# Sparse graph attention: shorter upper slot layers for eleven node tiles

## Chip, cores and metric

The kernel runs on one core of one Trainium2 chip. The metric is the device time of one execution in microseconds (us). The engines are PE (matrix multiply), DVE (vector), ACT (scalar, activation), POOL (GpSimd) and SP (sync, which only issues transfers here).

## What is computed

The input is `x` (4096 nodes, 128 features, float32) and an adjacency matrix `adj` (4096 x 4096, int32) with about 32 neighbours in a row. Two layers follow one another:

```
# layer 0: graph attention, 8 heads
Wh  = einsum('nd,hde->hne', x, W);  f1, f2 = Wh.a1, Wh.a2
e   = leaky_relu(f1[:, :, None] + f2[:, None, :], 0.2)
att = softmax(where(adj > 0, e, -9e15))
h   = elu(einsum('hnm,hmd->hnd', att, Wh))
x1  = layernorm(x + elu(concat_heads(h) @ W1 + b1))
# layer 1: per node and feature, quantiles (0.25, 0.5, 0.75) of x1
# over the kept neighbours, mean of the three, half mixed with x1, a linear layer, residual
```

Only the pairs where `adj` is set matter, so the kernel turns each row of `adj` into a list of neighbour numbers and fetches the rows that it needs.

## The kernel before

**Search.** `neighbours` (L550 and after) reads `adj` in tiles of 128 nodes, two loads of 1 MB each, makes keys from it on ACT and PE (L568, L607, L610), and takes the largest keys with DVE's MAX8 (L574, L579, L581). What comes out for a node is a record: 64 neighbour numbers, their count, the node's own number, `f1`, and the features. The work of one search is cut into pieces that are run between the parts of other work.

**Blocks.** The 32 tiles of nodes go through search and attention in three blocks of 4, 9 and 19 tiles (`BLOCKS`). Within a block the nodes are ranked by their neighbour count (`rank_by_count`, last instruction L750), and their records are scattered by rank into a DRAM array `recs_d` with one indirect transfer for each tile (L187, `rec_d<-rec,ranks`). A tile that is read back from there holds 128 nodes of nearly the same count, in rising order. While block b is in attention, the search of block b+1 runs between; its ranks are needed by the scatters that are placed among the last fetches of block b (`among` in `fetch_rows`).

**Slots and layers.** `CAPS` gives the largest count that each tile is laid out for. `layers(cap)` rounds it up to a multiple of 4 and splits it into layers of width 32, 16, 8 or 4. A layer of width w holds w slots of each of the 128 nodes; the 128 partitions of one gather then stand for 128/w nodes with w slots each, and w gathers cover the tile. A tile thus takes as many gathers as it has slots, each an indirect transfer of 128 rows of 136 floats (L178, `G<-xt_d,idx`) that POOL starts.

**Preparing a tile.** `read_lists` loads the tile's records `R` with four transfers by SP (L786), compares the count with the cap (L787; any node over it sets `bad`, and a general path then runs after all), and makes for each layer the index tile `idx` and the spread `f1x` on DVE. A layer of width 32 is transposed straight from `R` (L798). A narrower layer first gets four more transfers by SP into a buffer `narrow` (L806), one buffer for each width, then a copy `ids` (L808), a transpose (L811), a copy `f1b` (L815, the last reader of `narrow`) and a transpose `f1x` (L820).

**A step.** `step` handles one tile position i: it issues the fetch of tile i to POOL, runs `attend` for tile i-1 and the tail of `attend` for tile i-2, prepares tile i+2 after the first part of `attend`, and runs search pieces between the parts. The engines run in the order of the program text, so an instruction that waits holds all that follow it on its engine. `attend` adds `f1x` to the fetched scores (L869), exponentiates (L876), sums by node on PE (L883, `small`), takes the reciprocal (L894), spreads it back on PE (L898, `rz`), and for each layer builds the weights `wide` (L914) and multiplies the fetched rows by them, one matmul for each gather (L926, `y`). L883 and L898 take 32/w matmuls for a layer of width w. The fetched rows stand in a ring of six buffers `G` of 16 gathers; a buffer is free again when the `y` matmuls have read it.

**Layer 1.** After the last tile of attention, all `x1` rows are in DRAM, and POOL gathers neighbour rows again (L178, `vals`), while DVE runs a selection network on them (L1117).

The functions that the change touches:

Of the kernel before, what the change touches and what calls it, by code (L numbers as in the profile page):

```python
# [9 lines left out]
F32 = mybir.dt.float32  # L10
# [3 lines left out]
ALU = mybir.AluOpType  # L14
# [5 lines left out]
P = 128  # L20
N = 4096
D = 128
H = 8
# [20 lines left out]
CAPS = {  # L44
    4: [29, 33, 37, 60],
    9: [26, 28, 30, 32, 33, 35, 37, 40, 61],
    19: [24, 26, 27, 28, 29, 30, 30, 31, 32, 33, 33, 34, 35, 36, 37, 38, 40, 42, 62],
    32: [
        23, 24, 25, 26, 27, 27, 28, 29, 29, 30, 30, 30, 31, 31, 32, 32,
        33, 33, 34, 34, 35, 35, 36, 36, 37, 37, 38, 39, 40, 41, 44, 63,  # L50
    ],
}
BLOCKS = [4, 9, 19]


TURNS = {4: range(4), 9: range(9), 19: [0, 1, 2, 3, 18, 4, 5, 6, 7, *range(9, 18), 8]}

CAP = CAPS[NT]
# [15 lines left out]
R_NUM, R_OWN, R_F1 = L, L + 1, L + 2  # L74
# [10 lines left out]
def layers(c):  # L85


    out = []
    s = 0
    for w in (32, 32, 16, 8, 4):  # L90
        if (c + 3) // 4 * 4 - s >= w:
            out.append((s, w))
            s += w
    return out


def selection_network(n, targets):
# [104 lines left out]
def kernel(  # L202
# [15 lines left out]
    nc = tc.nc  # L218
# [3 lines left out]
    recs_d = [dram.tile([n * P, REC], F32, name=f"rec{n}_d") for n in BLOCKS]  # L222
# [5 lines left out]
    const = ctx.enter_context(tc.tile_pool(name="const", bufs=1))  # L228
# [6 lines left out]
    pidx = const.tile([P, 1], F32, name="pidx")  # L235
# [5 lines left out]
    for w in (32, 16, 8, 4):  # L241
        k = P // w
# [8 lines left out]
    for w in (32, 16, 8, 4):  # L251
        k = P // w // 4
# [13 lines left out]
    bad = const.tile([P, 5, NT], F32, name="bad")  # L266
# [17 lines left out]
    parts = adjp.tile([64, N], BF16, name="parts", bufs=1)  # L284
# [18 lines left out]
    with tc.tile_pool(name="setup", bufs=1) as sp, tc.tile_pool(  # L303
        name="setup_ps", bufs=2, space=PSUM
# [9 lines left out]
    attp = tc.alloc_tile_pool(name="att", bufs=2, reuse_waits="tile")  # L314
# [8 lines left out]
    narrow = {  # L323
        w: attp.tile([P, 32 // w, NARROW[w]], F32, name=f"narrow{w}", bufs=1) for w in NARROW
    }
    for v in narrow.values():
        nc.gpsimd.memset(v, 0.0)

    def prepare(b, i, t0):
        n = BLOCKS[b]  # L330
        i = TURNS[n][i]
        return read_lists(tc, attp, recs_d[b], i, CAPS[n][i], t0 + i, bad, narrow)

    ready = []

# [45 lines left out]
    t0 = 0  # L381
    with tc.manual_schedule(engines=ORDERED):
# [3 lines left out]
        for b, n in enumerate(BLOCKS):  # L386
            last = b == len(BLOCKS) - 1
            if last:
# [4 lines left out]
                idx = keep.tile([P, NT, L], I32, name="idx")  # L393
                cp = tc.alloc_tile_pool(name="cnt_all", bufs=2, side="right", reuse_waits="tile")
                pieces, left = None, 0
            else:
                pieces, left = search(t0 + n, BLOCKS[b + 1]), pieces_of(BLOCKS[b + 1])
            ready.append(prepare(b, 0, t0))
            for i in range(n):
# [6 lines left out]
                if not last and i == n - 1:  # L406
# [3 lines left out]
                    left = 0  # L410
# [12 lines left out]
                if last and i == n - 5:  # L423
                    R = cp.tile([P, NT, REC1], F32, name="R", bufs=1)
# [4 lines left out]
                    left = -(-LIST_PIECES // 4)  # L429
# [14 lines left out]
    with tc.tile_pool(name="sort", bufs=2) as sp, tc.tile_pool(name="fin", bufs=3) as fp, tc.tile_pool(  # L444
        name="fin_ps", bufs=2, space=PSUM
# [329 lines left out]
    return k  # L775


def read_lists(tc, ap, rec_d, i, cap, t, bad, narrow):


    nc = tc.nc

    R = ap.tile([P, REC], F32, name="R", bufs=5)
    rows = rec_d[ts(i, P), :]
    for u in range(4):
        nc.sync.dma_start(R[ts(u, 32), :], rows.rearrange("(g u) w -> u g w", u=4)[u])  # L786
    nc.vector.tensor_scalar(  # L787
        bad[:, 4, t : t + 1], R[:, R_NUM : R_NUM + 1], float(cap), None, ALU.is_gt
    )
    mine = ap.tile([P, 1], I32, name="mine", bufs=9)  # L790
    nc.vector.tensor_copy(mine, R.bitcast(I32)[:, R_OWN : R_OWN + 1])
    f1x32 = None
    parts = []
    for s0, w in layers(cap):
        k, e = P // w, 32 // w
        idx = ap.tile([P, 32], I32, name="idx", bufs=8)
        if w == 32:
            nc.vector.transpose(idx, R.bitcast(I32)[:, s0 : s0 + w])  # L798
            f1s = R[:, R_F1 : R_F1 + H].unsqueeze(1)
        else:  # L800

            v = narrow[w]
            words = R_X - s0
            src = rows.rearrange("(g i e) w -> i g e w", i=4, e=e)
            for j in range(4):
                nc.sync.dma_start(v[32 * j : 32 * j + w, :, 0:words], src[j, :, :, s0:R_X])  # L806
            ids = ap.tile([P, 32], I32, name="ids")
            nc.vector.tensor_copy(  # L808
                ids.rearrange("p (e s) -> p e s", e=e), v.bitcast(I32)[:, :, 0:w]
            )  # L810
            nc.vector.transpose(idx, ids)  # L811
            f1s = v[:, :, words - H : words]
        if w < 32 or f1x32 is None:
            f1b = ap.tile([P, H, 32], F32, name="f1b", bufs=1)
            nc.vector.tensor_copy(  # L815
                f1b.rearrange("p h (e s) -> p h e s", e=e),
                f1s.rearrange("p e h -> p h e").unsqueeze(3).to_broadcast([P, H, e, w]),
            )
            f1x = ap.tile([P, H * 32], F32, name="f1x", bufs=9)
            nc.vector.transpose(f1x, f1b.rearrange("p h g -> p (h g)"))  # L820
            if w == 32:
                f1x32 = f1x
        else:
            f1x = f1x32
        parts.append((s0, w, idx, f1x.rearrange("p (h g) -> p g h", h=H)[:, 0:w, :]))
    return R, mine, parts


def fetch_rows(tc, ap, lists, xt_d, among):

    nc = tc.nc
    R, mine, parts = lists
    out = []
    left = sum(w for _, w, _, _ in parts)
    G, col = None, 16
    for s0, w, idx, f1v in parts:
        runs = []
        for g in range(w):
            if col == 16:
                G, col = ap.tile([P, 16, XW], F32, name="G", bufs=6), 0  # L840
            if not runs or col == 0:
                runs.append([G, col, g, 0])
            runs[-1][3] += 1
            gather(nc, G[:, col, :], xt_d, idx[:, g : g + 1])
            col += 1
            left -= 1
            if among and left % 2 == 0 and left <= 2 * len(among) + 4:
                scatter(nc, *among.pop(0))
        out.append((w, P // w, runs, f1v))
    for v in among:  # L850
        scatter(nc, *v)
    return R, mine, out


def attend(tc, ap, pp, fetched, consts):


    nc = tc.nc
    R, mine, parts = fetched
    own, ownT = consts["own"], consts["ownT"]  # L860
    slots = sum(w for w, _, _, _ in parts)


    z = ap.tile([P, L, H], F32, name="z", bufs=2)
    layer = []
    a = 0
    for w, k, runs, f1v in parts:
        for G, col, g, m in runs:
            nc.vector.tensor_tensor(  # L869
                z[:, a + g : a + g + m, :], G[:, col : col + m, D:], f1v[:, g : g + m, :], ALU.add  # L870
            )
        layer.append(a)
        a += w
    zs = z[:, 0:slots, :].rearrange("p s h -> p (s h)")
    nc.vector.scalar_tensor_tensor(zs, zs, ALPHA, zs, ALU.mult, ALU.max)
    nc.scalar.activation(zs, zs, AF.Exp)  # L876
# [1 line left out]

    small = consts["small"]
    den = small[:, 0 : 32 * H]  # L880
    for i, (w, k, runs, f1v) in enumerate(parts):
        for r in range(k // 4):
            nc.tensor.matmul(  # L883
                den[0:4, :].rearrange("p (g r h) -> p r g h", r=k // 4, h=H)[:, r],
                lhsT=own[w][:, ts(r, 4)],
                rhs=z[:, layer[i] : layer[i] + w, :],
                start=(i == 0 and r == 0),
                stop=(i == len(parts) - 1),
                skip_group_check=True,
            )  # L890
# [2 lines left out]
    nc.vector.tensor_scalar(rden, den[0:4, :], TINY, None, ALU.max)  # L893
    nc.vector.reciprocal(rden, rden)  # L894
    rz = pp.tile([P, L * H], F32, name="rz")
    for i, (w, k, runs, f1v) in enumerate(parts):
        for r in range(k // 4):
            nc.tensor.matmul(  # L898
                rz[:, layer[i] * H : (layer[i] + w) * H],
                lhsT=ownT[w][:, r, :],  # L900
                rhs=rden.rearrange("p (g r h) -> p r g h", r=k // 4, h=H)[:, r],
                start=(i == 0 and r == 0),
                stop=(r == k // 4 - 1),
                skip_group_check=True,
            )
# [2 lines left out]

    y = pp.tile([P, 2, 512], F32, name="y")
    yf = y.rearrange("p a b -> p (a b)")  # L910
    for i, (w, k, runs, f1v) in enumerate(parts):
        pf = ap.tile([P, H * P], F32, name="wide")
        spread = [P, w, k, H]
        nc.vector.tensor_tensor(  # L914
            pf.rearrange("p (g k h) -> p g k h", g=w, k=k),
            z[:, layer[i] : layer[i] + w, :].unsqueeze(2).to_broadcast(spread),
            own[w].unsqueeze(1).unsqueeze(3).to_broadcast(spread),
            ALU.mult,
        )
        yield  # L920
        c = k * H
        for G, col, g0, m in reversed(runs):

            for g in reversed(range(g0, g0 + m)):

                nc.tensor.matmul(  # L926
                    yf[:, ts(g, c)],
                    lhsT=G[:, col + g - g0, 0:D],
                    rhs=pf[:, ts(g, c)],
                    start=(i == 0 and g % (w // 2) == w // 2 - 1),  # L930
                    stop=(i == len(parts) - 1),
                    skip_group_check=True,
                )
                if g % 8 == 0:
                    yield
# [455 lines left out]
```

## Time and profile before

| what | value |
|---|---|
| median of 3 runs | 3857.79 us (3854.88 to 3884.28) |
| profiled execution, own time | 3857.37 us |
| its span, from first to last instruction | 3855.5 us |
| POOL busy | 2807.9 us, 73% |
| DVE busy | 2671.4 us, 69% |
| PE busy | 1253.7 us, 33% |
| gathers `G`, attention | 1180, 947 ns median, 995 ns mean |
| gathers `vals`, layer 1 | 1024, 1382 ns mean |

Times in views of the trace are us from the start of the span. In a list of instructions in time, the columns are start, duration, engine, line, operation, operands, and in brackets how long the engine stood idle before it and what ended that. `issue` as a releaser is time in which the engine waited for nothing that the profile shows. In lists of waits the columns are total us, times and the longest single wait.

### The profile page before, as it was taken

The numbers are of one execution on the slowest core, as the hardware profiler recorded it, in microseconds if no ns is written. First come the engines' busy times: TensorE is split into PE (matmuls) and PEld (weight loads), VectorE is DVE, ScalarE is ACT, GpSimd is POOL, SyncE is SP. The second block draws the span as 40 slices with busy tenths as digits, with TensorE's granted clock in tenths as the row PEclk, the third lists the DMA queues.
The fourth block names the chain that finished last, engine by engine and source line by source line (L and its number), as shares of the span: only waits on it lengthen the run. The fifth ranks groups of instructions, "written<-read, shape, count | busy, mean of one in ns | idle before, by whom it ended". The sixth has DMA issues, their size and how long they took to land. (4 is left out here: it accounts for less than half of the span.)

```text
span 3855.5 us, 21960 instructions
## 1 busy us (share of the span) xinstructions
PE 1253.7 (33%) x5433; PEld 961.2 (25%) x5433; DVE 2671.4 (69%) x6439; ACT 403.4 (10%) x603; POOL 2807.9 (73%) x2388
## 2 busy tenths in 40 slices
PE   6483867863746444455600000000000000000001
PEld 2143534543635444444500000000000000000000
DVE  8774688782522222257436888669999999998788
ACT  3111223210111101111100000000000000000000
POOL 1657674577777777777478888877788887888882
PEclk9975666655665555555555555555555555555555
DMA  6423444322222222222111111111111111111110
GB/s 213 153 88 106 150 139 132 122 54 65 54 55 53 54 53 54 64 58 55 34 47 38 41 39 34 38 42 41 41 38 28 32 35 44 38 35 38 38 40 16
DMA packets 110281, 241.25 MB, mean 63 GB/s; under 512 B 46976, under 2 KB 63360, under 8 KB 101952
## 3 DMA queue, kind: packets, MB, share of 16 engines
q0 software_dynamic: 76160, 160.24, 15.3%
q10 hardware_dynamic: 9360, 67.18, 5.1%
q1 hardware_dynamic: 24624, 12.34, 1.3%
q8 instruction: 45, 0.74, 0.1%
q14 instruction: 92, 0.75, 0.1%
HBM read 228.44 MB, written 11.15 MB: 62 GB/s over the span
## 5 line engine op out<-in xcount | busy, mean ns | idle before, releaser
L178 POOL DMA_INDIRECT vals<-x_d,idx x1024 | 1415.6, 1382 | 314.4 <-issue 303.8
L178 POOL DMA_INDIRECT G<-xt_d,idx x1180 | 1173.6, 995 | 483.4 <-issue 339.9
L1117 DVE TENSOR_TENSOR work<-work 128x256 f32<-128x256 f32 (+7 forms) x1168 | 921.5, 823 | 0.7
L1137 PE MATMUL st_ps<-dg,goal 128*128 128x128 f32 x286 | 71.9, 429 | 1791.9 <-DVE goal L1117 1704.4
L1117 DVE TENSOR_TENSOR work<-work,work 128x512 f32<-128x512 f32 (+4 forms) x820 | 584.3, 738 | 1.3
L1137 PEld LDWEIGHTS st_ps<-dg,goal 128*128 128x128 f32 x286 | 63.7, 324 | 1798.4 <-issue 1797.5
L926 PE MATMUL y<-wide,G 128*128 128x32 f32 (+3 forms) x2360 | 480.1, 382 | 21.9 <-DVE wide L914 21.9
L926 PEld LDWEIGHTS y<-wide,G 128*128 128x128 f32 x2360 | 460.0, 297 | 45.8 <-DVE wide L914 24.2
L869 DVE TENSOR_TENSOR z<-G,f1x 128x128 f32<-128x128 f32 (+2 forms) x92 | 29.9, 335 | 471.6 <-DMA G<-xt_d,idx 468.5
L1117 DVE TENSOR_TENSOR work<-vals 128x768 f32<-128x768 f32 (+11 forms) x64 | 128.8, 2028 | 267.8 <-DMA vals<-x_d,idx 265.7
L574 DVE MAX8 first<-key 128x8 f32<-128x128 f32 x1024 | 227.5, 282 | 112.5 <-PE key L610 112.5
L607 PE MATMUL key<-sgn,markb 128*128 128x512 bf16 x256 | 142.0, 555 | 160.9 <-DVE first L574 107.5
L883 PE MATMUL small<-z,own 128*4 128x32 f32 (+3 forms) x436 | 50.4, 284 | 368.1 <-ACT z L876 368.1
L1136 ACT ACTIVATE dg<-ident,wt 128x128 f32<-128x128 f32 x143 | 47.5, 394 | 1105.0 <-PE st_ps L1137 1104.6
L568 ACT ACTIVATE sgn<-adj_t 128x2048 bf16<-128x2048 int32 x64 | 122.1, 1907 | 343.0 <-PE key L607 328.2
L898 PE MATMUL rz<-rden,ownT 4*128 4x32 f32 (+3 forms) x436 | 107.1, 419 | 117.9 <-DVE rden L894 96.5
L610 PE MATMUL key<-parts,oneb 64*128 64x512 bf16 x256 | 140.6, 550 | 6.3 <-POOL parts L196 6.3
L956 PE MATMUL small<-W_sb,late 128*128 128x128 f32 x512 | 118.9, 426 | 33.6 <-DVE late L953 33.6
L898 PEld LDWEIGHTS rz<-rden,ownT 4*128 4x128 f32 x436 | 94.5, 310 | 134.0 <-DVE rden L894 68.3
L187 POOL DMA_INDIRECT out_dram<-o,own_i x32 | 67.9, 2123 | 79.9 <-ACT o L1163 56.2
L883 PEld LDWEIGHTS small<-z,own 128*4 128x4 f32 x436 | 27.1, 102 | 385.8 <-ACT z L876 373.3
L956 PEld LDWEIGHTS small<-W_sb,late 128*128 128x128 f32 x512 | 110.2, 327 | 44.9 <-DVE late L953 43.9
(179 smaller groups left out, 1879.3 us busy)
## 6 DMA issues: line engine op xcount, KB each, us to landing
adj_t<-in_adj_dram ACTq DMA_DIRECT2D x64, 1024.0 KB
G<-xt_d,idx POOLq DMA_INDIRECT x1180
vals<-x_d,idx POOLq DMA_INDIRECT x1024
R<-rec_d SPq DMA_DIRECT2D x128, 26.2 KB
xt_d<-rec SPq DMA_DIRECT2D x4, 544.0 KB
rec<-in_x_dram SPq DMA_DIRECT2D x4, 512.0 KB
W_sb<-in_L_gnn_W_dram SPq DMA_DIRECT2D x2, 512.0 KB
a_b<-in_L_gnn_a_dram SPq DMA_DIRECT2D x2, 512.0 KB
```

What stands on the lines that cost most here:

```text
L178: nc.gpsimd.indirect_dma_start(out=dst, out_offset=None, in_=rows, in_offset=bass.IndirectOffsetOnAxis(ap=idx, axis=0),)
L187: return nc.gpsimd.indirect_dma_start(out=rows, out_offset=bass.IndirectOffsetOnAxis(ap=idx, axis=0), in_=src, in_offset=None,)
L568: nc.scalar.activation(sgn, adj_t, AF.Sign, accum_out=cnt[:, i : i + 1])
L574: nc.vector.max(first[:, ts(c0 // CW + c, 8)], key[:, ts(c, CW)])
L607: nc.tensor.matmul(key, lhsT=markb, rhs=sgn[:, ts(b, 512)], start=True, stop=False)
L610: nc.tensor.matmul(key, lhsT=oneb[0:64, :], rhs=parts[:, ts(r, 512)], start=False, stop=True)
L883: nc.tensor.matmul(den[0:4, :].rearrange("p (g r h) -> p r g h", r=k // 4, h=H)[:, r], lhsT=own[w][:, ts(r, 4)], rhs=z[:, layer[i] : layer ...
L898: nc.tensor.matmul(rz[:, layer[i] * H : (layer[i] + w) * H], lhsT=ownT[w][:, r, :], rhs=rden.rearrange("p (g r h) -> p r g h", r=k // 4, h ...
L926: nc.tensor.matmul(yf[:, ts(g, c)], lhsT=G[:, col + g - g0, 0:D], rhs=pf[:, ts(g, c)], start=(i == 0 and g % (w // 2) == w // 2 - 1), stop ...
L956: nc.tensor.matmul(o, lhsT=hv[:, h, :], rhs=consts["W1_sb"][:, h, :], start=(h == 0), stop=(h == H - 1))
L1117: nc.vector.tensor_tensor(slots_of(dst, (j, c, s, m), size), slots_of(a, (i, c, s, m), size), slots_of(b, (i + d, c, s, m), size), op,)
L1137: nc.tensor.matmul(st_ps[:, u, :], lhsT=goal[:, (j * k + u) * D : (j * k + u + 1) * D], rhs=dg, start=(j == 0), stop=False,)
```

## The change

A table `LAYERS` gives eleven tiles (block size, tile in the block) a list of layers of their own. Each entry has a third number g0: a layer with g0 > 0 fetches only gathers g0 to w-1, that is, the slots of the tile's last nodes. The other tiles keep `layers(cap)` with g0 = 0. For the adjacency that the reference draws, every node of these tiles has at least as many slots as neighbours.

```diff
+LAYERS = {
+    (4, 1): [(0, 32, 0), (32, 8, 7)],
+    (4, 2): [(0, 32, 0), (32, 4, 0), (36, 8, 7)],
+    (4, 3): [(0, 32, 0), (32, 16, 0), (48, 16, 15)],
+    (9, 0): [(0, 16, 0), (16, 8, 0), (24, 4, 2)],
+    (9, 4): [(0, 32, 0), (32, 4, 1)],
+    (9, 6): [(0, 32, 0), (32, 4, 0), (36, 4, 2)],
+    (9, 8): [(0, 32, 0), (32, 16, 0), (48, 16, 14)],
+    (19, 1): [(0, 16, 0), (16, 8, 0), (24, 4, 1)],
+    (19, 9): [(0, 32, 0), (32, 4, 2)],
+    (19, 17): [(0, 32, 0), (32, 8, 0), (40, 4, 1)],
+    (19, 18): [(0, 32, 0), (32, 16, 0), (48, 16, 13)],
+}
+def steps_of(parts):
+    held = [0] * P
+    for s0, w, g0 in parts:
+        for q in range(g0 * P // w, P):
+            if held[q] == s0:
+                held[q] += w
+    assert held == sorted(held)
+    return held[0], [(q, held[q] - held[q - 1]) for q in range(1, P) if held[q] > held[q - 1]]
...
+    nodeq = const.tile([P, 1], F32, name="nodeq")
+    for u in range(4):
+        nc.gpsimd.memset(nodeq[ts(u, 32), :], -float(P - 1) * u)
+    nc.vector.scalar_tensor_tensor(nodeq, pidx, 4.0, nodeq, ALU.mult, ALU.add)
...
+        parts = LAYERS.get((n, i)) or layers(CAPS[n][i])
...
-    nc.vector.tensor_scalar(
-        bad[:, 4, t : t + 1], R[:, R_NUM : R_NUM + 1], float(cap), None, ALU.is_gt
-    )
+    cap, rises = min(cap, steps_of(layer_list)[0]), steps_of(layer_list)[1]
+    over = R[:, R_NUM : R_NUM + 1]
+    for q, more in rises:
+        up = ap.tile([P, 1], F32, name="up", bufs=3)
+        nc.vector.tensor_scalar(up, nodeq, float(q), -float(more), ALU.is_ge, ALU.mult)
+        nc.vector.tensor_tensor(up, up, over, ALU.add)
+        over = up
+    nc.vector.tensor_scalar(bad[:, 4, t : t + 1], over, float(cap), None, ALU.is_gt)
...
-        for g in range(w):
+        for g in range(g0, w):
...
-        pf = ap.tile([P, H * P], F32, name="wide")
-        spread = [P, w, k, H]
+        k, n = P // w, w - g0
+        pf = ap.tile([P, H * P], F32, name="wide")
+        spread = [P, n, k, H]
```

The sums, the spreading back, the weights and the `y` matmuls of `attend` run over gathers g0 to w-1 in the same way. Each of the eleven tiles has one rise, so its check of the count takes two more small DVE instructions. The slots of these tiles, which are also their gathers, before and after, are:

| tile | widths before | gathers | widths after (gathers kept of the last layer) | gathers |
|---|---|---|---|---|
| (4,1) | 32, 4 | 36 | 32, 8 (1) | 33 |
| (4,2) | 32, 8 | 40 | 32, 4, 8 (1) | 37 |
| (4,3) | 32, 16, 8, 4 | 60 | 32, 16, 16 (1) | 49 |
| (9,0) | 16, 8, 4 | 28 | 16, 8, 4 (2) | 26 |
| (9,4) | 32, 4 | 36 | 32, 4 (3) | 35 |
| (9,6) | 32, 8 | 40 | 32, 4, 4 (2) | 38 |
| (9,8) | 32, 32 | 64 | 32, 16, 16 (2) | 50 |
| (19,1) | 16, 8, 4 | 28 | 16, 8, 4 (3) | 27 |
| (19,9) | 32, 4 | 36 | 32, 4 (2) | 34 |
| (19,17) | 32, 8, 4 | 44 | 32, 8, 4 (3) | 43 |
| (19,18) | 32, 32 | 64 | 32, 16, 16 (3) | 51 |

Tile (19,18) is fetched as the fifth of its block, (19,17) as the last but one.

More of the change, by code (lines that the diff above doesn't have):

```diff
@@ L91, in layers @@
         if (c + 3) // 4 * 4 - s >= w:
-            out.append((s, w))
+            out.append((s, w, 0))
             s += w
     return out
+def steps_of(parts):
[6 more added lines that the diff above has]
+    return held[0], [(q, held[q] - held[q - 1]) for q in range(1, P) if held[q] > held[q - 1]]
 def selection_network(n, targets):
@@ L331, in prepare @@
         i = TURNS[n][i]
-        return read_lists(tc, attp, recs_d[b], i, CAPS[n][i], t0 + i, bad, narrow)
+        parts = LAYERS.get((n, i)) or layers(CAPS[n][i])
+        return read_lists(tc, attp, recs_d[b], i, CAPS[n][i], parts, t0 + i, bad, narrow, nodeq)
     ready = []
@@ L775, in places, with read_lists @@
     return k
-def read_lists(tc, ap, rec_d, i, cap, t, bad, narrow):
+def read_lists(tc, ap, rec_d, i, cap, layer_list, t, bad, narrow, nodeq):
     nc = tc.nc
@@ L793, in read_lists @@
     parts = []
-    for s0, w in layers(cap):
+    for s0, w, g0 in layer_list:
         k, e = P // w, 32 // w
@@ L824, in read_lists @@
             f1x = f1x32
-        parts.append((s0, w, idx, f1x.rearrange("p (h g) -> p g h", h=H)[:, 0:w, :]))
+        parts.append((w, g0, idx, f1x.rearrange("p (h g) -> p g h", h=H)[:, g0:w, :]))
     return R, mine, parts
@@ L833, in fetch_rows @@
     out = []
-    left = sum(w for _, w, _, _ in parts)
+    left = sum(w - g0 for w, g0, _, _ in parts)
     G, col = None, 16
-    for s0, w, idx, f1v in parts:
+    for w, g0, idx, f1v in parts:
         runs = []
-        for g in range(w):
+        for g in range(g0, w):
             if col == 16:
@@ L841, in fetch_rows @@
             if not runs or col == 0:
-                runs.append([G, col, g, 0])
+                runs.append([G, col, g - g0, 0])
             runs[-1][3] += 1
@@ L848, in fetch_rows @@
                 scatter(nc, *among.pop(0))
-        out.append((w, P // w, runs, f1v))
+        out.append((w, g0, runs, f1v))
     for v in among:
@@ L860, in attend @@
     own, ownT = consts["own"], consts["ownT"]
-    slots = sum(w for w, _, _, _ in parts)
+    slots = sum(w - g0 for w, g0, _, _ in parts)
     z = ap.tile([P, L, H], F32, name="z", bufs=2)
@@ L866, in attend @@
     a = 0
-    for w, k, runs, f1v in parts:
+    for w, g0, runs, f1v in parts:
         for G, col, g, m in runs:
@@ L872, in attend @@
         layer.append(a)
-        a += w
+        a += w - g0
     zs = z[:, 0:slots, :].rearrange("p s h -> p (s h)")
@@ L880, in attend @@
     den = small[:, 0 : 32 * H]
-    for i, (w, k, runs, f1v) in enumerate(parts):
+    for i, (w, g0, runs, f1v) in enumerate(parts):
+        k = P // w
         for r in range(k // 4):
             nc.tensor.matmul(
-                den[0:4, :].rearrange("p (g r h) -> p r g h", r=k // 4, h=H)[:, r],
+                den[0:4, :].rearrange("p (g r h) -> p r g h", r=k // 4, h=H)[:, r, g0:],
                 lhsT=own[w][:, ts(r, 4)],
-                rhs=z[:, layer[i] : layer[i] + w, :],
+                rhs=z[:, layer[i] : layer[i] + w - g0, :],
                 start=(i == 0 and r == 0),
@@ L895, in attend @@
     rz = pp.tile([P, L * H], F32, name="rz")
-    for i, (w, k, runs, f1v) in enumerate(parts):
+    for i, (w, g0, runs, f1v) in enumerate(parts):
+        k = P // w
         for r in range(k // 4):
             nc.tensor.matmul(
-                rz[:, layer[i] * H : (layer[i] + w) * H],
+                rz[:, layer[i] * H : (layer[i] + w - g0) * H],
                 lhsT=ownT[w][:, r, :],
-                rhs=rden.rearrange("p (g r h) -> p r g h", r=k // 4, h=H)[:, r],
+                rhs=rden.rearrange("p (g r h) -> p r g h", r=k // 4, h=H)[:, r, g0:],
                 start=(i == 0 and r == 0),
@@ L910, in attend @@
     yf = y.rearrange("p a b -> p (a b)")
-    for i, (w, k, runs, f1v) in enumerate(parts):
+    for i, (w, g0, runs, f1v) in enumerate(parts):
+        k, n = P // w, w - g0
         pf = ap.tile([P, H * P], F32, name="wide")
-        spread = [P, w, k, H]
+        spread = [P, n, k, H]
         nc.vector.tensor_tensor(
-            pf.rearrange("p (g k h) -> p g k h", g=w, k=k),
-            z[:, layer[i] : layer[i] + w, :].unsqueeze(2).to_broadcast(spread),
+            pf[:, 0 : n * k * H].rearrange("p (g k h) -> p g k h", g=n, k=k),
+            z[:, layer[i] : layer[i] + n, :].unsqueeze(2).to_broadcast(spread),
             own[w].unsqueeze(1).unsqueeze(3).to_broadcast(spread),
@@ L921, in attend @@
         c = k * H
-        for G, col, g0, m in reversed(runs):
-            for g in reversed(range(g0, g0 + m)):
+        for G, col, a, m in reversed(runs):
+            for j in reversed(range(a, a + m)):
+                g = g0 + j
                 nc.tensor.matmul(
                     yf[:, ts(g, c)],
-                    lhsT=G[:, col + g - g0, 0:D],
-                    rhs=pf[:, ts(g, c)],
+                    lhsT=G[:, col + j - a, 0:D],
+                    rhs=pf[:, ts(j, c)],
                     start=(i == 0 and g % (w // 2) == w // 2 - 1),
```

## Prediction

> **What bounds the kernel now.** I read the page first (busy tenths and costliest groups), then POOL's waits by stage, and last POOL's and DVE's instructions in time where a wait ends. The chain that ended last on the page reaches back only about 30 us, so it says nothing of the attention. From the page:
>
> ```profile
> DVE  8774688782522222257436888669999999998788
> POOL 1657674577777777777478888877788887888882
> L178 POOL DMA_INDIRECT vals<-x_d,idx x1024 | 1415.6, 1382 | 314.4 <-issue 303.8
> L178 POOL DMA_INDIRECT G<-xt_d,idx x1180 | 1173.6, 995 | 483.4 <-issue 339.9 <-PE y L926 99.8 <-DVE v L984 14.5
> ```
>
> POOL is the busiest engine, and the 0.3 us of "issue" before each gather is its own as well (339.9 / 1114 waits). So a gather costs about 1.28 us of POOL: the stretch from 1087.8 to 1157.1 holds 54 gathers, 69.3 / 54. But 53 gathers less are worth 53 x 1.28 = 67.8 us only where POOL is what ends last. The waits of POOL tell where. From 365 to 850 us, which is block 1, and then from 934 to 1885, which is block 2:
>
> ```profile
> POOL G L178 <- PE y L926: 77.3, 6, 32.4
> POOL G L178 <- DVE v L984: 14.5, 1, 14.5
> POOL G L178 <- PE key L607: 7.3, 1, 7.3
> POOL rec_d L187 <- DVE ranks L750: 0.4, 1, 0.4
> ...
> POOL G L178 <- issue: 196.1, 643, 0.3
> POOL all_d L187 <- issue: 9.8, 32, 0.3
> POOL G L178 <- PE y L926: 0.9, 3, 0.3
> ```
>
> In block 2 POOL never waits longer than 0.3 us. In block 1 it waits 99 us for ring buffers, because PE and DVE are held by the search of block 2. The other direction settles it; DVE's waits from 365 to 850 us:
>
> ```profile
> DVE first L574 <- PE key L610: 76.5, 38, 7.0
> DVE ids L808 <- DMA R<-rec_d: 10.0, 1, 10.0
> ```
>
> DVE never waits for a gather `G` there. Search, not POOL, sets block 1. Now the ends of blocks 0 and 1, where POOL meets the ranks (POOL and DVE in time):
>
> ```profile
> 307.54 0.17 DVE L750 CAST ranks<-rank 128x8 int32<-128x8 f32 x1
> 847.19 0.17 DVE L750 CAST ranks<-rank 128x8 int32<-128x8 f32 x1
> ...
> 271.36 0.95 POOL L178 DMA_INDIRECT G<-xt_d,idx  x1 [21.57 <-PE y L926]
> 322.04 1.00 POOL L187 DMA_INDIRECT rec_d<-rec,ranks  x1 [0.31 <-DVE v L978]
> 817.36 0.96 POOL L178 DMA_INDIRECT G<-xt_d,idx  x1 [4.97 <-PE y L926]
> 847.64 1.00 POOL L187 DMA_INDIRECT rec_d<-rec,ranks  x1 [0.38 <-DVE ranks L750]
> ```
>
> In block 0 the ranks are ready 14.3 us before POOL wants them (322.04 against 307.71). In block 1 they are ready at 847.36 and POOL scatters at 847.64: POOL already waits for them, by 0.08 us. Whatever POOL saves before this point in block 1 is waited away.
>
> **What the Trainium skill says.** "DMA: Bandwidth & Descriptors", section "Issuing engine by pattern", gives indirect transfers to GpSimd alone; the trace agrees, all 1180 are on POOL, so none can move. "Perfetto Trace Analysis", section "Optimization Strategy", says that the most contended engine can change over a kernel's regimes and that its gaps should be followed to the semaphore that ends them; the 99 us of block 1 against none in block 2 are such regimes. "DMA: Bandwidth & Descriptors", section "Issuing engines are not separate DMA queues", says that transfers of all issuers interleave on the same 16 engines; the 10.0 us wait above, right behind three 1 MB loads of `adj`, agrees, against 1.8 us for a `narrow` load without such loads.
>
> **The change part by part.**
>
> *Block 0* loses 3 + 3 + 11 = 17 gathers. The six of tiles (4,1) and (4,2) come before the wait that ends at 271.36, so they only lengthen it. That release needs PE's `y` of tile (4,1), whose step began with `z` at 231.05, 32 us after that tile's last gather was issued: search sets it. The search gets: in step 0, tile (4,2) with one more narrow layer, 0.14 + 0.21 + 0.25 + 0.45 = 1.05 us of DVE, about 1 us of wait as its width 8 buffer was just read for (4,1), and four small instructions of 0.15; in step 1, tile (4,3) with two layers of width 16, where the second load of the one buffer must wait for the first `f1b`, minus one layer. Such a reload shows in block 2 (SP issues at 936.26 and DVE copies at 939.79): 3.5 us, for four issues and landing. Together +5 us. Against it, tile (4,1) has 5 instead of 9 sums and spreads each, and a matmul here counts as two passes: 8 passes of 4.47 / 18 = 0.25 us for `rz` and 0.08 for `small` = -2.6 us before the release. Net +2: release at 273.5. Then 27 gathers instead of 38 (the scatters start when 22 are left) take 34.6 us: POOL at 308. The ranks move little (+2, minus a `wide` of 1.2 and 7 us of PE's `y` for which DVE waits only in part): 308. So the scatters start at 309.5 instead of 322.04: **-12.5 us**, and everything behind them is unchanged.
>
> *Block 1* loses 2 + 1 + 2 + 14 = 19 gathers, 24 us of POOL, and I count none of them: with 14 gathers less before the scatters POOL reaches the ranks some 20 us early and stands there. What counts is how the search moves.
> - Step 0 attends to (4,3): 5 instead of 15 sums and spreads. 20 passes of `rz` less at 6.57 / 30 = 0.22 us and 20 of `small` at 0.065 are 5.7 us, for which DVE now waits 7.0 us; `y` loses 7.8 us of PE, and `wide` 2.3 us of DVE. Taken: -9, as part of the `y` is hidden by MAX8.
> - Step 7 attends to (9,6): 17 instead of 5 sums and spreads, 24 passes more of each, 24 x 0.285 = +6.8; one more half `wide`, 0.6. Taken: +6, a key or two being ready ahead.
> - (9,6) and (9,8) each reload one buffer at once: 3.5 us each, and add three narrow layers, 3 x 1.05, minus a transpose of 0.2. The check of the count adds 2 x 0.15 for each of three tiles. Sum 10.9; a pause of DVE lets PE catch up, which later saves part of the 76.5 us of waits for PE. Taken: +8.
> - (9,0) and (9,4) spare 0.9 us of `wide` and some PE: -1.
>
> Sum +4, rounded up to **+5 us** at the ranks. After them the same 42 gathers and 19 scatters follow.
>
> *Block 2* loses 1 + 2 + 1 + 13 = 17 gathers where POOL never waits: 17 x 1.28 = **-21.8 us**. Tile (19,18) adds two narrow layers and a reload, some 6 us of DVE in step 2, but DVE is busy 36% of 847 to 1885 us, and POOL is two tiles ahead; without that cover it would cost these 6 us. Each of the eleven tiles takes as many ring buffers of 16 as before (64 and 51 gathers both need 4), so the order in which buffers are reused stays. The last tile and the 45 us from the last gather at 1885 to the first `vals` at 1930 are unchanged. The extra SP issues, 20 at about 0.4 us, lie on a queue that mostly waits.
>
> *Set-up*: four memsets and one DVE instruction, under 1 us, while POOL waits 73 us for ranks: nothing.
>
> *Layer 1*, 1930 to 3855, only moves.
>
> Sum: -12.5 + 5 - 21.8 = -29.3 us. From the profiled 3857.37 that is 3828.1, and the profiled run lies 0.4 us below the median of the runs shown: I say **3828 us**, 0.8% faster. What this measurement can tell from no change is about 1%, or 38.6 us.
>
> **Costs not shown.** The reload under loads of `adj`: below, 1 us, when SP is quick and the landing is half covered; above, the 10.0 us of the row quoted; I take 3.5. With four of them, this is -10 to +26 us on the sum. The PE time of small passes: between 0 and twice what I took, plus or minus 7 us around steps 0 and 7.
>
> **Rivals.**
> 1. *Every gather pays.* If the search turns out to be pulled along by POOL, all 53 count: 3857.4 - 67.8 = 3790. For it: POOL is the busiest engine and step 0's relief on PE is large. Against it: DVE has no wait for `G` in block 1, and the ranks' 0.38 us. Half-way, a search that gains 15 us more than I count, gives 3813.
> 2. *Reloads behind the adjacency.* The four immediate reloads of `narrow`, (4,2), (4,3), (9,6) and (9,8), stop DVE, and with it the queue of MAX8 on which PE's keys, ACT's signs and the ranks depend. At the 10.0 us seen, they cost 40 instead of the 11.5 counted, +28.5; if PE's 6.8 us and the layers also come in full, some +5 more: 3828 + 34 = 3862, slower than before. It decides from 11 us a reload. For it: loads of `adj` run all through blocks 0 and 1. Against: that wait followed three loads issued at once, while later ones come singly.
> 3. *Block 2 is paid elsewhere.* If DVE's lists for layer 1, which run in the last four steps at about 80% DVE, or the ring ends block 2, its 21.8 us vanish: 3850.
> 4. *The tables don't hold*, so that `bad` sends the kernel through the general path, with a time many times as long. The lists of the reference's adjacency fit, so I give it next to nothing.
>
> **How the numbers follow.** Forecast, 3815 to 3843: 0.66. Rival 1 with its half-way: 0.14. Rival 3: 0.10. Rival 2: 0.09. Rival 4: 0.01. The limits at 1% are 3819 and 3896. Faster: rival 1 and 0.06 of the forecast's low tail, 0.20. Slower: 0.04, from a rival 2 at more than twice its price and rival 4. Same: 0.76. The range takes the forecast and reaches into rivals 1 and 3: 3811 to 3850.
>
> **What would show it.** Right: the first `rec_d` scatter of block 0 near 309; in block 1 a POOL wait of about 20 us on the ranks before the first scatter, near 840; block 2 without waits and 22 us shorter; 1127 gathers `G` at the same 947 ns; `ids` waits for `narrow` of about 3 us in the prepares of (4,3), (9,6), (9,8). Wrong: the ranks of block 1 before 830 (rival 1), or after 860 with `ids` waits of 10 us (rival 2), or new POOL waits after 930 (rival 3).

## Result and the profile after

| | kernel before | kernel after |
|---|---|---|
| median | 3859.46 us (20 runs) | 3845.89 us (20 runs) |
| ratio after / before | | 0.9969, 95% interval 0.9954 to 0.9983 |
| span of the profiled execution | 3855.5 us | 3841.0 us |
| gathers `G` | 1180 | 1127 |

A ratio of 0.9969 is 12 us of 3859 less, where the forecast was 29.3. A second series gave 0.9964 (0.9952 to 0.9976), and a second trace with it, called "again" below.

The page of the kernel after, the rows that answer to those of before (busy tenths, then the two costliest groups of POOL):

```profile
DVE  8785778772522222256446879769999999998788
...
POOL 1657763457777777777478788887788887888882
...
L205 POOL DMA_INDIRECT vals<-x_d,idx x1024 | 1423.3, 1390 | 314.3 <-issue 300.8
L205 POOL DMA_INDIRECT G<-xt_d,idx x1127 | 1121.0, 995 | 496.6 <-issue 320.6
```

One gather still takes 995 ns in the mean; POOL is busy 52.6 us less with `G` and stands idle 13.2 us more ahead of them. Where, is seen in POOL's waits. In block 1, 347 to 849 us:

```profile
POOL G L205 <- PE y L969: 104.5, 6, 35.8
POOL G L205 <- issue: 78.0, 256, 0.3
POOL G L205 <- DVE rstd L1035: 16.9, 1, 16.9
```

In block 2, 932 to 1865 us:

```profile
POOL G L205 <- issue: 188.6, 619, 0.3
POOL all_d L214 <- issue: 9.4, 31, 0.3
```

Block 2 has no wait over 0.3 us, as before. In block 1 POOL waits for ring buffers as before, and more. DVE's waits in the same stretch of block 1:

```profile
DVE first L607 <- PE key L643: 85.3, 38, 6.4
DVE ids L847 <- DMA narrow<-rec_d: 16.0, 6, 5.8
```

DVE still never waits there for a gather, but it waits for `narrow`: 2.41 us for the second layer of (9,6), 5.77 us for that of (9,8), and two waits of 3.5 us at the start of the block, where the kernel before has its one wait of 10.0 us. The ends of blocks 0 and 1, DVE's and POOL's instructions in time:

```profile
303.86 0.17 DVE L783 CAST ranks<-rank 128x8 int32<-128x8 f32 x1
848.61 0.17 DVE L783 CAST ranks<-rank 128x8 int32<-128x8 f32 x1
...
304.31 1.00 POOL L214 DMA_INDIRECT rec_d<-rec,ranks  x1 [2.87 <-DVE rk L774]
849.06 1.00 POOL L214 DMA_INDIRECT rec_d<-rec,ranks  x1 [20.48 <-DVE ranks L783]
```

The scatters of block 0 start 17.7 us earlier than before (322.04), those of block 1 1.4 us later (847.64), after a wait of 20 us in which POOL does nothing. So block 1, measured from its predecessor's first scatter to its own, grew from 525.6 to 544.75 us. The stages of all traces from series in which the kernel before takes 3859 to 3861 us (first scatter of block 0; block 1 as just defined; block 2 from there to the first `vals`; layer 1 from there to the start of the last store), in us:

| kernel | scatter of block 0 | block 1 | block 2 | layer 1 |
|---|---|---|---|---|
| before | 322.0 | 525.6 | 1082.6 | 1920.3 |
| before, again | 319.4 | 526.2 | 1078.7 | 1926.6 |
| after | 304.3 | 544.8 | 1057.7 | 1925.4 |
| after, again | 304.5 | 550.1 | 1060.8 | 1922.5 |
| entries of blocks 0 and 2 only | 304.4 | 521.1 | 1058.2 | 1915.6 |
| own memory for a second layer | 303.5 | 532.4 | 1059.5 | 1930.2 |
| without (9,6) and (9,8) | 309.2 | 519.8 | 1058.8 | 1921.0 |
| only (9,8) | 319.1 | 533.4 | 1078.2 | 1922.2 |
| only (9,6) | 320.1 | 536.3 | 1075.3 | 1923.4 |
| own memory, without (9,6) and (9,8) | 303.9 | 528.6 | 1059.6 | 1924.4 |

With its entries block 0 ends some 16 us sooner and block 2 is some 21 us shorter, in every kernel that has them (in one trace block 0 ends at 309.2 instead of 304; why isn't shown). Block 1 is where some 20 us were lost. Layer 1 scatters by some 6 us between traces of one kernel, so no difference there is read.

### The profile page after: what moved, and what is told of

It reads as the page before. It is cut to its first block, busy times and chain, and to the rows that moved or that the text cites. A ratio compares the mean times of both kernels' runs of the same rounds, so it can differ in the third digit from the quotient of the medians.

```text
span 3841.0 us, 21855 instructions
## 1 busy us (share of the span) xinstructions
PE 1237.5 (32%) x5375; PEld 943.6 (25%) x5375; DVE 2673.4 (70%) x6484; ACT 403.4 (11%) x603; POOL 2760.4 (72%) x2339
## 5 line engine op out<-in xcount | busy, mean ns | idle before, releaser
L205 POOL DMA_INDIRECT G<-xt_d,idx x1127 | 1121.0, 995 | 496.6 <-issue 320.6
L969 PE MATMUL y<-wide,G 128*128 128x32 f32 (+2 forms) x2254 | 455.9, 381 | 23.1 <-DVE wide L956 23.1
L969 PEld LDWEIGHTS y<-wide,G 128*128 128x128 f32 x2254 | 435.4, 295 | 47.2 <-DVE wide L956 26.0
L908 DVE TENSOR_TENSOR z<-G,f1x 128x128 f32<-128x128 f32 (+5 forms) x93 | 29.2, 327 | 430.4 <-DMA G<-xt_d,idx 429.3
L923 PE MATMUL small<-z,own 128*4 128x32 f32 (+6 forms) x460 | 48.7, 270 | 337.7 <-ACT z L915 337.7
L939 PE MATMUL rz<-rden,ownT 4*128 4x32 f32 (+6 forms) x460 | 109.9, 406 | 132.2 <-DVE rden L934 110.4
L988 PE MATMUL hT<-late,W_sb 128*128 128x128 f32 x512 | 109.1, 399 | 40.3 <-ACT late L982 40.3
```

Of the source, the lines that this page charges most:

```text
L205: nc.gpsimd.indirect_dma_start(out=dst, out_offset=None, in_=rows, in_offset=bass.IndirectOffsetOnAxis(ap=idx, axis=0),)
L939: nc.tensor.matmul(rz[:, layer[i] * H : (layer[i] + w - g0) * H], lhsT=ownT[w][:, r, :], rhs=rden.rearrange("p (g r h) -> p r g h", r=k // ...
L969: nc.tensor.matmul(yf[:, ts(g, c)], lhsT=G[:, col + j - a, 0:D], rhs=pf[:, ts(j, c)], start=(i == 0 and g % (w // 2) == w // 2 - 1), stop= ...
L988: nc.tensor.matmul(hT[:, ts(h, P)], lhsT=consts["W_sb"][:, h, :], rhs=yT[:, h, :], start=True, stop=True)
```

## Experiments

The theory: in block 1 the search (DVE and PE) sets the time, gathers saved there are waited away, and what the entries of block 1 add to DVE lengthens it. The main rival: every gather pays its 1.28 us of POOL wherever it is saved.

### Parts of the table

Four kernels with only some of the entries. They ran in a series in which the kernel before took 4469.73 us, and each ratio is against it there.

Only block 2:

```diff
-    (4, 1): [(0, 32, 0), (32, 8, 7)],
...
-    (9, 8): [(0, 32, 0), (32, 16, 0), (48, 16, 14)],
     (19, 1): [(0, 16, 0), (16, 8, 0), (24, 4, 1)],
...
```

> The table keeps only the four tiles of block 19, 17 gathers less. Search theory (block 1 is set by the search, block 2 by POOL): the ranks of block 1 stay at 847 us, block 2 is 22 us shorter, and the whole is 22 us faster, ratio 0.9943. Paid-back theory (what the attention gains is partly lost in layer 1 and at the end, as the profile of the full change shows some 9 us longer there): 13 us faster, 0.9966. Every-gather theory (each removed gather pays 1.28 us wherever it stands): 22 us too.

Measured: 0.9969 (0.9949 to 0.9989), 14 us less. The theory's 0.9943 lies outside the interval, the 0.9966 of the paid-back theory in it.

Only block 1, in the same way:

> The table keeps only the four tiles of block 9, 19 gathers less. Search theory: the gathers pay nothing, POOL stands some 20 us before the first scatter of block 1, and the search gets longer by the narrow layers and reloads of (9,6) and (9,8) and the sums of (9,6): ranks at 864 to 868 us instead of 847, the whole 17 to 21 us slower, ratio 1.0049. Clock theory (the later ranks of the full change came from a lower granted clock and not from its tables): within 5 us of before. Every-gather theory: 24 us faster, 0.9937.

Measured: 1.0021 (1.0000 to 1.0042). Nineteen gathers less, and not faster; the 0.9937 of every gather is far outside. The theory's 1.0049 is too high as well. POOL stood 20.41 us at the ranks, and block 1 of this trace took 750 us, against 708 to 713 in the traces of the other three kernels.

Only block 0:

> The table keeps only the three tiles of block 4, 17 gathers less. Search theory: the first scatter of block 0 at 304 us instead of 322, step 0 of block 1 another 3 us shorter, ranks of block 1 near 826, the whole 20 us faster, ratio 0.9948. Paid-back theory: 11 us, 0.9972. Every-gather theory: 22 us.

Measured: 0.9941 (0.9923 to 0.9959), 26 us less. That excludes the paid-back theory, but not every gather, which forecasts nearly the same.

Blocks 0 and 2, without block 1:

> The table keeps blocks 4 and 19 and drops the four tiles of block 9: 34 gathers less, 19 more than the full change. Search theory: the two gains add up, ranks of block 1 near 826 us, the whole 40 to 44 us faster than before, ratio 0.989, and so about 28 us faster than the full change. Every-gather theory: slower than the full change by 24 us. Paid-back theory: 33 us faster than before.

Measured: 0.9913 (0.9884 to 0.9942), 39 us less, about the sum of the two parts, 14 + 26. This series differs from the first in block 2. DVE's waits and one of POOL's in the kernel with block 1's entries alone, from 1180 to 2500 us:

```profile
DVE rden L926 <- remote: 421.1, 10, 55.3
DVE rden L926 <- PE small L916: 172.6, 7, 60.4
...
POOL G L198 <- PE y L962: 243.9, 12, 27.8
```

There DVE stops ten times for 42 us in the mean at the reciprocal of a tile, and POOL waits twelve times for the `y` of a tile, 20 us in the mean. So POOL alone is not the bound of block 2 in that series, and the sizes don't carry over; the signs do.

### The same where the kernel before takes 3860 us

The kernel after once more, as a second trace and series:

> The full change once more, for a second trace of it beside the others. Search theory: in the trace the ranks of block 1 come again within 3 us of before's or later, though block 0 ends some 18 us sooner, and block 2 is 22 us shorter; ratio 0.994 to 0.998. Paid-back theory: layer 1, from the first vals to the last store, is again about 5 us longer than the 1921 us of before. If that is chance, it lies anywhere from 1914 to 1927.

Measured: 0.9964 (0.9952 to 0.9976), 3848.28 us; block 1 took 550.1 us. Layer 1 took 1922.5 us, so nothing is paid back there.

Blocks 0 and 2 only:

> Blocks 4 and 19 only, again, beside the full change on the same chip. Search theory: 0.989 to 0.991 of before, some 20 to 28 us faster than the full change with 19 gathers more, because block 9's table only lengthens the search. Every-gather theory: 24 us slower than the full change.

Measured: 0.9920 (0.9897 to 0.9943), 3828.37 us. It issues 19 gathers more than the kernel after and is 20 us faster. That every gather pays is refuted; the entries of block 1 cost time.

### Memory of its own for the second layer of a width

(4,3), (9,6), (9,8) and (19,18) have two narrow layers of one width. In the kernel after, the second load must wait until `f1b` has read the first. Here it goes into memory of widths that these tiles don't use. For this the buffers of widths 16 and 8 are joined in one tile; all buffers together are as large as before, and nothing else changes:

```diff
+    narrow[16, 2] = cut(n16, 2, R_X - 48)
+    narrow[4, 2] = cut(0, 8, R_X - 36)
...
-            v = narrow[w]
+            again = [p[1] for p in layer_list if p[0] < s0].count(w) > 0
+            v = narrow[w, 2] if again else narrow[w]
```

> The full change, but the second layer of the same width in one tile is loaded into memory of its own, so that its four transfers no longer wait for the first layer's copy. Search theory with reloads as the cause: the waits of 2.4 to 5.8 us of the ids copies in (4,3), (9,6) and (9,8) go, the ranks of block 1 come 8 to 12 us sooner, the whole 8 to 12 us faster than the full change, ratio near 0.994. If the reloads are hidden anyway and the narrow layers' own instructions and PE's sums are the cause: under 3 us.

Measured: 0.9918 (0.9897 to 0.9939), 3832.53 us, with all 53 gathers saved. The waits in block 1 for a second layer are gone, and the block takes 532.4 instead of 544.8 and 550.1 us. That is more than the 8 to 12 us expected, and more than the two waits, 8.2 us together. What such a wait does is seen in the step that prepares (9,8). The kernel after, DVE in time:

```profile
726.30 0.18 DVE L847 COPY ids<-narrow 128x32 int32<-128x32 int32 x1 [5.77 <-DMA narrow<-rec_d]
```

The waits of DVE and of PE in that step (716.8 to 783.6 us):

```profile
DVE first L607 <- PE key L643: 9.3, 4, 3.0
DVE ids L847 <- DMA narrow<-rec_d: 5.8, 1, 5.8
...
PE key L640 <- DVE first L607: 15.2, 5, 11.0
```

With own memory, the same step (705.3 to 766.3 us):

```profile
DVE first L614 <- PE key L650: 9.0, 4, 2.6
...
PE key L647 <- DVE first L614: 7.8, 5, 5.2
```

PE's next `key` needs a buffer that DVE's MAX8 (`first`) has read. While DVE stands 5.8 us at `ids`, PE runs out of buffers and stands too: its longest wait for `first` grows from 5.2 to 11.0 us, by the length of the stop. Over the step DVE waits for keys just as much as without the stop (9.3 against 9.0 us). Nothing is caught up.

### Without the two entries of block 1 that add layers

```diff
-    (9, 6): [(0, 32, 0), (32, 4, 0), (36, 4, 2)],
-    (9, 8): [(0, 32, 0), (32, 16, 0), (48, 16, 14)],
```

> The full change without tiles (9,6) and (9,8), which have layers split further: 16 gathers more. Search theory: these two cost about 20 us of the search (7 in the step that prepares (9,6), 9 in the one that prepares (9,8), 4 in the one that attends to (9,6)), so the ranks of block 1 come near 826 us and the whole is some 20 us faster than the full change, ratio 0.990, like blocks 4 and 19 alone. Clock theory (chance in PE's clock): as the full change. Every-gather theory: 20 us slower than the full change.

Measured: 0.9915 (0.9894 to 0.9936), 3826.38 us. POOL issues 16 gathers more than in the kernel after, and waits at the ranks of block 1 for

```profile
828.97 1.00 POOL L212 DMA_INDIRECT rec_d<-rec,ranks  x1 [0.39 <-DVE ranks L781]
```

only 0.39 us. The scatter after the ranks starts 20 us earlier than in the kernel after (849.06). Of block 1's entries these two are what costs; (9,0) and (9,4) do no harm.

### Each of the two by itself

The kernel before with the one entry (9,8), and with the one entry (9,6):

> The kernel before with the one table entry of tile (9,8): 14 gathers less, all ahead of the ranks of block 1. Theory (the search sets block 1, and a narrow layer that must be fetched again stops it): the step that prepares (9,8) takes 66 to 67 us instead of 58, of which 5 to 6 us is the wait for the second layer of width 16; block 1, from its first scatter of the block before to its own, takes 534 us instead of 525.6, POOL waits some 20 us at the ranks, and the time is 8 to 9 us longer, a ratio near 1.002. Rival (every gather pays 1.28 us): 18 us shorter, 0.995.

Measured: 1.0010 (0.9992 to 1.0028); block 1 533.4 us, its step that prepares (9,8) 66.2 us instead of 58.4, the wait at `ids` 5.7 us, the wait of POOL 19.85 us:

```profile
735.67 0.18 DVE L837 COPY ids<-narrow 128x32 int32<-128x32 int32 x1 [5.71 <-DMA narrow<-rec_d]
...
852.49 1.00 POOL L204 DMA_INDIRECT rec_d<-rec,ranks  x1 [19.85 <-DVE ranks L773]
```

The stage is as the theory said, and 0.995 lies outside the interval: fourteen gathers less brought nothing. That the whole got slower isn't shown, as the interval holds 1. DVE and PE in the step that prepares (9,8), in the kernel before (its second trace) and then in this one:

```profile
DVE first L574 <- PE key L610: 8.4, 4, 2.4
PE key L607 <- DVE first L574: 5.2, 5, 2.8
...
DVE first L597 <- PE key L633: 8.5, 4, 3.2
PE key L630 <- DVE first L597: 15.8, 6, 11.0
```

PE waits 10.6 us more for DVE, and DVE waits for PE as much as before: here too nothing is caught up.

> The kernel before with the one table entry of tile (9,6): 2 gathers less, a third layer, and 17 instead of 5 sums and spreads. Theory: the step that prepares it takes 57 to 58 us instead of 51.3, the step that attends to it 69 to 73 instead of 64.3, so block 1 takes 537 to 540 us instead of 525.6 and the kernel 11 to 15 us longer, a ratio near 1.0035. Rival (only the wait of 2.4 us and the gathers count): block 1 within 2 us of before, ratio 1.000.

Measured: 1.0010 (0.9994 to 1.0025); block 1 536.3 us, just under the 537 to 540 expected, so that the rival's "within 2 us" falls in the trace. In the total time I expected too much: 1.0035 lies above the interval, and the rival's 1.000 in it. The preparing step took 60.6 us, more than the 57 to 58 expected, and the one after it 57.2 instead of 62.1. With this goes the column before the last but one, PE's granted clock. The kernel before (its second trace), steps 4 and 5; columns are the stretch, its length, busy time of PE, PEld, DVE, ACT, POOL (with instructions), the clock, the DMA share and GB/s:

```profile
613.93:665.33 51.40, 35.97 (x138) 21.09 (x138) 47.04 (x186) 15.09 (x17) 22.63 (x25) 0.63 0.42 129
665.33:727.43 62.10, 48.41 (x184) 29.93 (x184) 46.35 (x184) 18.00 (x19) 22.95 (x24) 0.61 0.39 127
```

The kernel with only (9,6), the same steps:

```profile
614.46:675.06 60.60, 40.89 (x138) 23.32 (x138) 48.76 (x192) 15.06 (x17) 23.27 (x25) 0.56 0.36 111
675.06:732.26 57.20, 42.14 (x184) 26.21 (x184) 46.20 (x184) 17.90 (x19) 20.61 (x21) 0.71 0.42 136
```

The same 138 matmuls take PE 36.0 us at a clock of 0.63 and 40.9 at 0.56, and the same 184 take 48.4 at 0.61 and 42.1 at 0.71. Single steps are therefore not to be read alone; the four steps 3 to 6 together are 229.2 us against 225.0.

### Both cures, and the kernel before again

Own memory for the second layer and without (9,6) and (9,8):

> The changed kernel without the entries of (9,6) and (9,8), and with memory of its own for the second narrow layer of a width. Theory: in block 1 no layer is fetched again any more, so the own memory is worth only the 1 us of block 0 here; block 1 takes 518 to 521 us, the time is within 3 us of the kernel that only leaves out the two entries, ratio 0.991. Rival (own memory is worth its 16 us anywhere, through where the buffers lie): ratio 0.987.

Measured: 0.9877 (0.9848 to 0.9906), 3818.33 us in 5 runs, the fastest of all. The theory's 0.991 lies just outside the interval, and the rival's 0.987 in it. The interval overlaps that of leaving out the two entries alone, and the two ran in different series, so it isn't settled whether own memory gains something even where block 1 has no layer to fetch again; the rival stays open. The trace, of the slowest of the five runs, shows no such gain: its block 1 took 528.6 us, 7.6 over the upper end expected. The first three steps took 196.3 us instead of the 189.2 of the kernel that only leaves out the two entries, at a lower clock (0.52 against 0.57 in the first). Its steps 3 and 4:

```profile
545.90:601.75 55.85, 40.94 (x138) 22.94 (x137) 47.03 (x186) 16.20 (x17) 25.00 (x27) 0.56 0.38 121
601.75:658.10 56.35, 40.74 (x138) 23.32 (x138) 47.37 (x187) 15.03 (x17) 23.25 (x25) 0.56 0.39 118
```

The kernel before needs 53.0 us at 0.60 and 51.4 at 0.63 for them, although here no entry of the table adds work for DVE or PE in these two steps.

> The kernel before once more, for a second trace of it: block 1 from first scatter to first scatter takes 525.6 us within 3, its eight steps within 1.5 us each of the first trace. If steps differ by more than that from one execution to the next, then differences of some us in single steps are chance, and only the sums over steps can be read.

Measured: 526.2 us, and the sum of the eight steps 485.8 against 485.2. Six steps agree within 0.2 us; the first two differ by 2.5 and 1.7 in opposite directions, more than the 1.5 expected. Here too the clock of the first was lower (0.57 against 0.59).

## Why the prediction was right or wrong

The direction was right and the time lies inside the range, but the change brought less than half of what was forecast, 12 us of 29.3. The table has the steps of the sum, with the mean of the two traces of before (320.7, 525.9, 1080.7, 1923.4 us) against the two of after. Step k of block 1 prepares tile (9,k+2) and attends to (9,k-1), step 0 to (4,3); its length is taken between the starts of DVE's leaky ReLU on `z` (L875, after the change L914) of two tiles.

| step of the sum | forecast | measured |
|---|---|---|
| block 0, to the first scatter | -12.5 | -16.4, -16.2 |
| block 1 | +5 | +18.8, +24.2 |
| of this, steps 0 to 2: (4,3), (9,0), (9,4) | -10 | -6.4, -1.1 |
| of this, steps 3 to 6: reloads and layers | +8 | +19.8, +15.6 |
| of this, step 7: attends to (9,6) | +6 | +4.4, +8.5 |
| block 2 | -21.8 | -22.9, -19.9 |
| layer 1 | 0 | +1.9, -0.9 |

- **Block 0**: right in kind. The release of the ring did not come later, at 273.5, but at 267.99, and the ranks at 303.86 instead of 308. POOL then waited 2.87 us for them (1.62 us in the second trace): the search, not POOL, now ends this block too. That the block brought 4 us more than forecast is luck.
- **Block 2 and layer 1**: right. No wait of POOL over 0.3 us, 17 gathers for 22.9 and 19.9 us. The reload of (19,18) stopped DVE for 3.4 us, but POOL did not wait for it.
- **Gathers of block 1 worth nothing**: right. The wait of 20 us at the ranks is there (20.48), and it is the same 20 us with (9,8)'s entry alone (19.85), without any gain in time.
- **The failed step is the sum for block 1, "+5": the mechanism was right, but two of its terms were mis-sized.** It missed the measured block by 14 and 19 us. The first term accounts for some 4 us of that, the second for 5 and 7; the rest is open.
- **First term: "a pause of DVE lets PE catch up, which later saves part of the 76.5 us of waits for PE. Taken: +8."** Nothing is saved later. With one entry at a time, the stop and DVE's added work came through in full. For (9,8): a wait of 5.7 us and 1.8 us more of DVE in the step make 7.5, and the four steps grew by 7.9. For (9,6): 2.5 + 1.7 = 4.2, and they grew by 4.2, though as +9.2 in one step and -5.0 in the next, so that this agreement may be chance. That is 12.1 for both, where +8 was taken. The price of one reload was a mean of 4.1 us, 2.41 and 5.77, not 3.5.
- **Second term: step 0, "Taken: -9"**, too large. The step got 1 to 5 us shorter. PE had 51 matmuls less to do in it (247 to 196), and `rz` shrank as forecast, from 6.6 and 6.1 us to 2.7 and 1.6. But `y` took 20.9 and 22.5 us instead of 22.0 and 23.8, not 7.8 less. DVE saved 2 us of its own work and waited for keys 14.8 and 16.3 us instead of 15.8 and 18.1, so little of PE's relief reached it.
- **What stays open.** Steps 3 to 6 of the full change lost 3.5 to 7.7 us beyond the 12.1. Of this, 2.8 us are in step 3, where no entry has work. In steps 3 to 5 of the two traces PE's clock is 0.56, 0.59, 0.58 and 0.56, 0.59, 0.61, where before has 0.60, 0.63, 0.61. The kernel with both cures has the same 55.8 us and 0.56 in step 3, and 56.3 us and 0.56 in step 4, with no reload or added layer there. So this excess need not come from the two entries; what sets the clock isn't shown. For the same reason own memory, which leaves the layers and took the four steps from +19.8 and +15.6 to +3.1, can't be credited with all of that.
- **Step 7, +6**: right. With (9,6)'s entry alone it is 70.2 against 64.2.

DVE's waits for keys in step 0, before (366.94 to 439.20 us) and after (350.38 to 419.74 us):

```profile
DVE first L574 <- PE key L610: 15.8, 7, 7.0
...
DVE first L607 <- PE key L643: 14.8, 7, 3.2
```

Of the rivals, the first (every gather pays) is refuted by the kernels that issue more gathers and are faster. The second (reloads behind the adjacency, 10 us each) named the right mechanism but too large a price: it needed 11 us a reload, and the waits for a second layer of one width were 2.46, 2.41 and 5.77 us. The third (block 2 paid elsewhere) is refuted by the 21 us of block 2 where the kernel before takes 3860 us; in the slower series POOL had long waits in block 2, but the entries of block 2 still brought 14 us there. The fourth played no part.

## What to carry to other kernels

Before counting instructions saved on the busiest engine, go through its waits stage by stage: here 17 gathers less were worth 21 us in one block and 19 less were worth nothing in another, where the engine waits for someone else. In the stage that another engine sets, look at what the change adds to *that* engine, and count a stop in the middle of a producer and consumer pair in full: here the partner ran out of buffers and stopped too. A buffer used twice in a row turns a transfer that was hidden into such a stop; other memory for the second use brought 16 us here, and leaving out the two tiles that need it 22 us (why own memory brought more than the waits it removes is open).

## What the runs showed of the hardware

The granted clock of PE differs from step to step in one execution, from 0.57 to 0.73 in block 1 of the second trace of before, and between executions in a step with the same work (0.60 and 0.56 in step 3, which took 53.0 and 55.8 us). The same 138 matmuls took PE 36.0 us at 0.63 and 40.9 at 0.56. Where PE and DVE work hand in hand a step with unchanged work moved by 5 us with it (62.1 and 57.2), as much as whole terms of the sum, and two traces of one kernel differ by 5 us in a block (544.8 and 550.1).

In one series the kernel before took 4469.73 us, against 3859 to 3861 in the others, and the trace of the kernel with block 1's entries alone has stops of some 42 us of DVE at one line there. Their cause isn't shown by the trace, which names it only `remote`. Whether the chip itself was slower isn't shown either: the record gives the same chip number to that series and to the next one, in which the kernel before took 3860.26 us.
